# A perceiver block on one core: the sums' spread set later in its step, and a tail with loads on GpSimd, shared eT copies and split feed-forward products

## The chip, the cores and the metric

One core of a Trainium2 chip runs the whole block. The metric is the device time of one launch in microseconds. Three runs of the kernel before gave 1708.46 us in the median (1707.39 to 1709.91). In this text PE is the matrix engine (TensorE), DVE is VectorE, ACT is ScalarE, POOL is GpSimd, and SP is the engine that only issues transfers; "SPq" marks its queue.

## The reference

Eight batches of 64 latents of width 512 pass through cross attention to 1601 context rows (16 heads of 128), causal self attention over the latents (16 heads of 32) and a gated feed-forward with ternary weights. The residual sums carry through.

```python
def xattn(h, enc):                      # h: (8, 64, 512), enc: (8, 1601, 256)
    q, k, v = heads(h @ Wq), heads(enc @ Wk), heads(enc @ Wv)
    q, k = rmsnorm(q, gq), rmsnorm(k, gk)
    a = softmax(einsum('bqhd,bkhd->bhqk', q, k) / sqrt(128))
    return einsum('bhqk,bkhd->bqhd', a, v).reshape(B, S, -1) @ Wo

def attn(x):                            # causal, 16 heads of 32
    q, k, v = split(x @ w_attn + b_attn)
    a = softmax(where(tril, q @ k.T * 32 ** -0.5, -inf))
    return (a @ v) @ w_proj + b_proj

def ffn(x):
    gate, up = split(x @ ternary(w_gate_up).T)
    return rms_norm(silu(gate) * up) @ ternary(w_proj).T

x = x + xattn(layernorm(x), ctx)
x = x + attn(layernorm(x))
x = x + ffn(layernorm(x))
```

## The kernel before

**The loop.** The long middle part, from about 125 to 1398 us, is a loop of 16 *units* (eight batches times two groups of eight heads), each of six *steps* (`step(u, q)`, q from 0 to 5). A step takes two tiles of 128 context rows, makes their keys and scores by Strassen-like products (`product`, line 573, on the PSUM tiles `p_u`, `p_5`, `s_a`, `p_2`, `s_2`), and meanwhile finishes the softmax of the unit before and weighs the context with it (`weigh_context`, line 668, PSUM `y0`, `y1`). The order of the instructions of PE, DVE, ACT and POOL in this loop is the order in which they stand in the program. In the sixth step the row sums of the unit before are complete: `find_sum` (line 676) splits `den` into `denh` (ACT) and `denl` (DVE), and `spread_sum` (line 682) multiplies both by a matrix of ones on PE (line 110, PSUM `bp`) and copies the result to `rB` (ACT). `invert_sums` (DVE) takes its reciprocals later in the step. Before, `spread_sum` stands behind `tail_scores` (line 526, PSUM `sp`) and ahead of `p_5`. `bp`, `p_5` and `p_2` share the PSUM tag `m`, which has two buffers.

**The tail of cross attention** (lines 955 to 1004). Here only PE's order is written by hand; the order on the other engines and queues is the planner's. PE weighs the last unit's 13 context tiles (line 668). Their loads `cxn` (line 159) go out on SP, five buffers deep, each when PE has finished with a buffer. SP also issues 16 `wo` loads of 256 KB (line 733), `wa_qk` of 2 MB (line 989), `x_again` of 1 MB (line 971) and two `wa_vp` of 1 MB (lines 993 and 996).

**Self attention** (from line 1212). `t` counts four tiles of 128 latents (two batches each), `rp` two pairs of heads' quarters. A list `todo` holds filler work for PE with a rough cost in us: output projections of cross attention (`op`, line 754), `turn` (transposes of the normalised rows, line 1079, copied to `xT_a`), `queries_and_keys` (`mm_qk`, line 1100), `own_values` (`mm_v`, line 1118). `fill(us)` runs as much of it as the number says. The eight attention pieces (t, rp) run between: `own_scores` (`spa`, line 1136; softmax on DVE and ACT, line 1161), `own_weighted` (transposes `tp_e`, line 1184; copies `eT` on ACT, line 1186; products `oTp`, line 1193), `own_projection` (copy `oT`, line 1203; `mm_p`, line 1207; sum `x2` on DVE, line 1211). Transposes take the PSUM tag `m` (two buffers), scores `k` (two), projections and values `s` (two).

**The feed-forward.** `split_turn` normalises a tile of `x2`, transposes it and keeps it as `xT_f` (ACT, fp32r) and `xT_lo` (DVE, the rest). `gate_or_up` (line 1315, PSUM `gu`) multiplies 128 rows of the gate or up weights by both, eight matmuls for each. Sixteen rounds `r` follow, then the output products `fop` (line 1383), scaled and added in `fy` (line 1399) and stored by SP (line 1402). The weights `fgu` and `fp` are loaded from POOL's queue (2 MB each).

Of the kernel before, what the change touches and what calls it, by code (L numbers as in the profile page):

```python
# [14 lines left out]
ALU = mybir.AluOpType  # L15
# [13 lines left out]
def perceiver_kernel(  # L29
# [700 lines left out]

    def load_wo(h):
        wo_sb[h] = piece("wo", h in (0, H - 1))
        nc.sync.dma_start(wo_sb[h], wo[ts(h, HD), :])

    def values(h, tag):
        g, hg = divmod(h, HG)
# [48 lines left out]
    def step(u, q):  # L785
# [43 lines left out]
            exponentials(u - 1, js)  # L829
        if q == NQU - 1:  # L830
            tail_scores(u)
            if u > 0:
                spread_sum(u - 1)


        p_5 = bank("p_5")
# [7 lines left out]
        product(s_a[:, 0], s1, v1, True)  # L844
        product(s_a[:, 1], a11, q11, False)
        nc.scalar.copy(half[:, 1:3], s_a)
        product(p_u, s2, t2_, False)
        u2 = kept("u2")
        nc.scalar.copy(u2, p_u)
# [105 lines left out]
    with tc.manual_schedule(engines={mybir.EngineType.PE}):  # L955

        later.pop()()
        wv_sb.append(load_wv(1))
        for jw in range(NJ - LAG, NJ):
            load_contexts((last - 1) * NJ + jw + CXN)  # L960
            weigh_context(last - 1, jw)
        find_max(last)
        mB[last] = spread_diag(mB[last])
        finish(last - 1)
        for h in range(HG // 2):
            values(h, "k")
# [4 lines left out]
        nc.sync.dma_start(x_sb, xf.rearrange("(t p) d -> p t d", p=P))  # L971
# [17 lines left out]
        nc.sync.dma_start(  # L989
            wa_qk, w_attn[:, 0 : 2 * D].rearrange("(c p) n -> p c n", p=P)  # L990
        )
        wa_vp = big.tile([P, 2, ND, D], F32, tag="A", name="wa_vp")
        nc.sync.dma_start(
            wa_vp[:, 0], w_attn[:, 2 * D :].rearrange("(c p) n -> p c n", p=P)
        )
        nc.sync.dma_start(wa_vp[:, 1], w_aproj.rearrange("(c p) n -> p c n", p=P))
        finish(last)


        x1 = x_sb  # L1000
        ops = {0: ps.tile([P, D], F32, tag="s", name="op")}
        project(ops[0], 0, range(HG))
        for h in range(HG, H):
            values(h, "k")
# [65 lines left out]
            nc.vector.tensor_tensor(x1[:, t, :], ops.pop(t), x_sb[:, t, :], ALU.add)  # L1070
            xns[t] = normalise(x1, t, aw_)

    def turn(t, hi, lo=None):


        xn = xns.pop(t)
        tp = ps.tile([P, ND, P], F32, tag="m", name="tp_ln")
        for c in range(ND):
            nc.tensor.transpose(tp[:, c, :], xn[:, ts(c, P)], ident)
        if lo is None:  # L1080
            nc.scalar.copy(hi[:, :, ts(t, P)], tp)
        else:
            nc.scalar.copy(hi[:, :, ts(t, P)], tp)
            for c in range(ND):
                nc.vector.tensor_tensor(
                    lo[c][:, ts(t, P)],
                    tp[:, c, :],
                    hi[:, c, ts(t, P)].bitcast(F32),
                    ALU.subtract,
                )  # L1090
# [21 lines left out]
            ALU.add,  # L1112
        )

    def own_values(t):
        mm = ps.tile([P, D], F32, tag="s", name="mm_v")
        for c in range(ND):
            nc.tensor.matmul(
                mm,
                xT_a[:, c, ts(t, P)],  # L1120
                wa_vp[:, 0, c, :],
                start=(c == 0),
                stop=(c == ND - 1),
            )
        nc.vector.tensor_tensor(v_sb[:, t, :], mm, bv, ALU.add)

    probs, oTp = {}, {}

# [46 lines left out]
    def own_weighted(t, rp):  # L1175
# [4 lines left out]
        for r in rs:  # L1180
            e = probs.pop((t, r))
            tp = ps.tile([P, ND, P], F32, tag="m", name="tp_e")
            for j in range(ND):
                nc.tensor.transpose(tp[:, j, :], e[:, j, :], ident)
            eT[r] = aw_.tile([P, ND, P], F32, tag="eT", name="eT")
            nc.scalar.copy(eT[r], tp)
        yield
        if rp == 0:
            oTp[t] = ps.tile([P, ND, P], F32, tag="y0", name="oTp", bufs=1)
# [23 lines left out]
    with tc.manual_schedule(engines={mybir.EngineType.PE}):  # L1213
# [53 lines left out]
        put(0.0, load_fgu, 1)  # L1267
        put(3.4, own_values, 3, name="v3")

        def split_turn(t):  # L1270
            xns[t] = normalise(x2, t, aw_)
            turn(t, xT_f, xT_lo)

        pieces = [divmod(i, 2) for i in range(2 * NTT)]

        def scores_of(i):
            if i < len(pieces):
                if pieces[i][0] > 1:
                    need(f"qk{pieces[i][0]}")
                own_scores(*pieces[i])  # L1280

        scores_of(0)
        for i, (t, rp) in enumerate(pieces[:-2]):
            fill(2.0)
            scores_of(i + 1)
            fill(1.5)
            if t:
                need(f"v{t}")
            run(own_weighted(t, rp), 1.5)
            if i == len(pieces) - 3:  # L1290
                scores_of(i + 2)
            if rp == 1:
                run(own_projection(t), 1.5)
        need("v3")

        xT_f = blk([P, ND, NT], "xT_f", FR)
        xT_lo = [
            piece("xT_lo", False, FR) for _ in range(ND)
        ]
        xs_ = [xT_f[:, c, :] for c in range(ND)], xT_lo  # L1300
        load_fgu(NF // 8 + 1)
        for t in range(NTT - 2):
            put(0.5, split_turn, t)
        t = NTT - 1
        run(own_weighted(t, 0), 0.5)
        fill(1e9)
        run(own_weighted(t, 1), 0.5)
        split_turn(t - 1)
        run(own_projection(t), 0.5)

        def gate_or_up(gu, i, r, cols):
            rr = r + i * NF
            for c in range(ND):
                for n_ in range(2):
# [38 lines left out]

        acc = aw_.tile([P, NT], F32, tag="oT", name="acc", bufs=1)
        for r in range(NF):
            gu = gu0
            if r:
                gu = [ps.tile([P, NT], F32, tag=n_, name="gu") for n_ in ("k", "s")]  # L1360
                for i in range(2):
                    gate_or_up(gu[i], i, r, slice(0, NT))
# [13 lines left out]
                    load_fp(k)  # L1376
        for t in range(NTT):
            op = ps.tile([P, D], F32, tag="m", name="fop")
            for r in range(NF):

                w_r = fp_sb[r // 8][:, r // 4 % 2 * 4 : r // 4 % 2 * 4 + 4, r % 4, :]
                for n_ in range(2):
                    nc.tensor.matmul(  # L1383
                        op,
                        hT[r][n_][:, ts(t, P)],
                        w_r,
                        start=(r == 0 and n_ == 0),
                        stop=(r == NF - 1 and n_ == 1),
                    )
            if t == 0:  # L1390
                ss = ps.tile([P, NTT], F32, tag="y0", name="ss", bufs=1)
                for k in range(NTT):
                    nc.tensor.matmul(
                        ss[:, k : k + 1], acc[:, ts(k, P)], ones, start=True, stop=True
                    )
                inv = small.tile([P, NTT], F32, tag="inv", name="inv", bufs=1)
                rsqrt_into(inv, ss, 1.0 / FF, eps32_t)
            y = t2([P, D], "fy")
            nc.vector.scalar_tensor_tensor(
                y, op, inv[:, t : t + 1], x2[:, t, :], ALU.mult, ALU.add  # L1400
            )
            nc.sync.dma_start(outf[ts(t, P), :], y)


# [41 lines left out]
```

## Time and profile before

| | |
|---|---|
| median of three runs | 1708.46 us |
| the profiled run | 1706.96 us |
| its span | 1705.1 us |
| PE busy in 400 to 500, 500 to 600 us | 100.00, 99.51 |
| PE busy in 1418 to 1430 (12 us) | 10.28 |
| PE busy in 1514 to 1583 (69 us) | 66.51 |
| PE busy in 1583 to 1619 (36 us) | 30.05 |
| DMA engines busy, moved, in 1418 to 1430 | 0.92, 321 GB/s |
| DMA engines busy, moved, in 1491 to 1514 | 0.00, 0 GB/s |

A line of the timeline gives the start in us from the span's start, the length, the engine, the line of the program, the operation, the tiles written and read, the shape, how many, and in brackets how long the engine sat idle before it and what released it. The records of neighbouring matmuls overlap, because they are pipelined: a list that gives starts says more about PE's pace than the lengths. "Waits" lines give the waiting engine and line, what it waited for, the total us, how many times, and the longest.

### The profile page before, as it was taken

What the parts mean: (1) busy time and instruction counts of PE and PEld (TensorE: products, weight loads), DVE (VectorE), ACT (ScalarE), POOL (GpSimd) and SP (SyncE); (2) the same over time, 40 slices, a digit from 0 to 9 for tenths busy, and PEclk for the clock granted to TensorE, in tenths of its full rate; (3) what the DMA queues carried; (4) which work ended last, traced back from release to release, by engine and by line L of the source; (5) the groups of instructions that cost most, each with busy time, mean ns of one, the idle gap of its engine ahead of it and who ended that gap; (6) DMA issues with size and microseconds to landing.
All of it is one profiled execution on the core that took longest, in us unless ns stands there. A gap on an engine that the chain in (4) does not pass through costs nothing.

```text
span 1705.1 us, 19635 instructions
## 1 busy us (share of the span) xinstructions
PE 1675.0 (98%) x5288; PEld 929.4 (55%) x5288; DVE 1185.2 (70%) x1896; ACT 1148.2 (67%) x4487; POOL 413.0 (24%) x538
## 2 busy tenths in 40 slices
PE   8999999999999999999999999999999999999899
PEld 3445455555555555555555555555555554466687
DVE  4446778787888878787878787888878785145431
ACT  4448787878787777777787878787777763023441
POOL 1001232324232323132232324232333120100031
PEclk9999999999999999999999999999999999999999
DMA  7002122212221122222222212221121126400330
GB/s 213 1 0 41 28 51 45 47 41 53 44 52 41 41 55 43 47 43 48 47 44 45 47 41 53 44 52 41 41 55 49 46 71 232 108 0 1 99 99 25
DMA packets 257623, 92.59 MB, mean 54 GB/s; under 512 B 210128, under 2 KB 236264, under 8 KB 257512
## 3 DMA queue, kind: packets, MB, share of 16 engines
q1 hardware_dynamic: 250698, 78.48, 19.8%
q0 software_dynamic: 6240, 12.58, 2.8%
q8 instruction: 42, 0.69, 0.2%
q14 instruction: 69, 0.57, 0.1%
q10 hardware_dynamic: 574, 0.27, 0.1%
HBM read 77.62 MB, written 7.34 MB: 50 GB/s over the span
## 4 chain that ended last, share of the span: by engine, by line
PE 92%; DVE 4%; ACT 2%; DMA 1%; issue 0%; SPq 0%; DVEq 0%
PE y L668 20%; PE p_u L573 19%; PE p L573 14%; PE s_a L573 14%; PE gu L1315 3%; PE qps L346 3%; PE op L754 3%; PE s L573 2%; PE fop L1383 2%; PE mm_qk L1100 2%; PE vp L739 2%; PE kp L262 2%; PE aps L372 2%; PE sp L526 1%; PE bp L110 1%; ACT e L1161 1%
## 5 line engine op out<-in xcount | busy, mean ns | idle before, releaser
L577 ACT ACTIVATE c<-c 128x128 f32<-128x128 f32 x1152 | 340.7, 297 | 140.4 <-DVE c L874 58.5
L668 PE MATMUL y<-s,cxn 128*128 128x512 f32 x768 | 356.7, 592 | 1.7 <-DMA cxn<-in_ctx_dram 1.7
L668 PEld LDWEIGHTS y<-s,cxn 128*128 128x128 f32 x768 | 144.7, 190 | 153.1 <-issue 136.6
L577 ACT ACTIVATION_READ_ACCUMULATOR c<-c 128x1 f32 x1152 | 215.5, 187 | 0.0
L655 POOL TENSOR_TENSOR den<-den,s 128x512 f32<-128x512 f32 x150 | 190.8, 1272 | 43.4 <-ACT s L646 36.4
L573 PEld LDWEIGHTS s_a<-aT,cxS 128*128 128x128 f32 x576 | 109.3, 190 | 137.9 <-issue 123.3
L573 PE MATMUL s_a<-aT,cxS 128*128 128x256 f32 x576 | 171.3, 379 | 0.0
L862 POOL COPY gate<-mx 128x1 f32<-128x1 f32 x60 | 11.1, 185 | 618.3 <-DVE mx L561 287.1
L547 DVE TENSOR_TENSOR s<-s,ssq 128x1024 f32<-128x1024 f32 x96 | 116.9, 1218 | 24.3 <-ACT ssq L105 24.2
L646 ACT ACTIVATE s<-s,zero_t 128x1024 f32<-128x1024 f32 (+1 forms) x117 | 115.9, 991 | 4.6 <-DVE s L642 4.6
L642 DVE TENSOR_TENSOR s<-s,mB 128x1024 f32<-128x1024 f32 (+1 forms) x117 | 116.5, 1018 | 2.2 <-ACT mB L620 2.1
L563 DVE TENSOR_TENSOR mx<-mx,s 128x512 f32<-128x512 f32 x160 | 111.1, 694 | 7.6
L874 DVE TENSOR_TENSOR c<-p_u,p 128x512 f32<-128x512 f32 x96 | 65.4, 681 | 71.4 <-PE p_u L573 71.4
L899 DVE TENSOR_TENSOR s<-s_a,half 128x512 f32<-128x512 f32 x96 | 66.2, 690 | 58.7 <-POOL den L655 41.0
L577 ACT ACTIVATE p_u<-p_u 128x128 f32<-128x128 f32 x384 | 99.9, 260 | 9.1
L573 PE MATMUL p_u<-wkS,cxT 128*128 128x512 f32 x192 | 98.3, 594 | 2.6 <-DVE c L874 2.6
L573 PE MATMUL p_u<-wkS,cxS 128*128 128x512 f32 x192 | 98.2, 593 | 0.4 <-ACT p L810 0.4
L573 PE MATMUL p<-wk,cxS 128*128 128x512 f32 x192 | 98.3, 594 | 0.0
L573 PE MATMUL p<-wkS,cxS 128*128 128x512 f32 x192 | 98.2, 593 | 0.0
L573 PE MATMUL p_u<-wk,cxS 128*128 128x512 f32 x192 | 98.0, 592 | 0.0
L573 PE MATMUL p<-wk,cxT 128*128 128x512 f32 x192 | 98.0, 592 | 0.0
L573 PE MATMUL p_u<-wk,cxT 128*128 128x512 f32 x192 | 98.0, 592 | 0.0
(202 smaller groups left out, 3164.3 us busy)
## 6 DMA issues: line engine op xcount, KB each, us to landing
cxn<-in_ctx_dram SPq DMA_DIRECT2D x192, 128.0 KB
cxB<-in_ctx_dram SPq DMA_DIRECT2D x192, 64.0 KB
wf<-in_L_ffn_w_gate_up_dram SPq DMA_DIRECT2D x32, 256.0 KB
fgu<-fw POOLq DMA_DIRECT2D x4, 2048.0 KB, 8.5
fw<-wT SPq DMA_DIRECT2D x192, 32.0 KB
wq<-in_L_xattn_Wq_dram SPq DMA_DIRECT2D x4, 1024.0 KB
wf<-in_L_ffn_w_proj_dram SPq DMA_DIRECT2D x16, 256.0 KB
wo<-in_L_xattn_Wo_dram SPq DMA_DIRECT2D x16, 256.0 KB
```

What stands on the lines that cost most here:

```text
L346: nc.tensor.matmul(qps, wq_sb[h // 4][:, c, ts(h % 4, HD)], xT[:, c, :], start=(c == 0), stop=(c == ND - 1),)
L547: nc.vector.tensor_tensor(flat, flat, kr.unsqueeze(2).to_broadcast([P, 2 * HG, S]), ALU.mult)
L563: nc.vector.tensor_tensor(mx[u][:r], mx[u][:r], s[:r], ALU.max)
L573: nc.tensor.matmul(out_, a, w, start=start, stop=True, skip_group_check=not start)
L577: nc.scalar.activation(k[:, ts(h, HD)], k[:, ts(h, HD)], AF.Square, accum_out=ssq[:, 4 * half + h : 4 * half + h + 1],)
L642: nc.vector.tensor_tensor(t, t, m.to_broadcast([r, len(js), W]), ALU.subtract)
L646: nc.scalar.activation(t, t, AF.Exp, bias=zero_t[: t.shape[0]], scale=1.0)
L655: eng.tensor_tensor(den[u][:r], den[u][:r], s[:r], ALU.add)
L668: nc.tensor.matmul(yps[u][c], cxn[u, j][:r, ts(c, P)], s[:r], start=(j == 0), stop=(j == NJ - 1),)
L754: nc.tensor.matmul(op, o_sb[h][:, ts(t, P)], wo_sb[h], start=(h == 0), stop=(h == H - 1),)
L874: nc.vector.tensor_tensor(c22, p_u, p5, ALU.add)
L899: nc.vector.tensor_tensor(quarters[:, 1::2], s_a, half[:, 0:2], ALU.add)
```

## The change

1. In the sixth step `spread_sum` moves from behind `tail_scores` to behind the first `s_a` products and their copy `half`.
2. `wo`, `x_again`, `wa_qk` and both `wa_vp` are loaded from POOL's queue instead of SP's.
3. `turn(0)` and `turn(1)` run ahead of the last pair of heads of `out_projection(2)`. `own_values(2)` is cut into two halves of 256 columns, with `turn(3)` between them.
4. Of the two `eT` copies of a piece, the second goes to DVE.
5. The last three attention pieces are written out by hand: all remaining filler runs ahead of piece (2,1); scores of (3,1) stand between the transposes and the products of (2,1); the turns of feed-forward tiles 0 and 1 stand in the projection of tile 2; and the products of the first two feed-forward rounds (`first(r, i, a, e)`: round r, gate or up i, column tiles a to e) run in pieces of 128 and 256 columns between the last attention steps. `turn(2)` uses the PSUM tag `y1`.
6. The last output tile is made in two halves of 256 columns, each scaled and stored by itself.

```diff
     def load_wo(h):
-        nc.sync.dma_start(wo_sb[h], wo[ts(h, HD), :])
+        nc.gpsimd.dma_start(wo_sb[h], wo[ts(h, HD), :])
...
         if q == NQU - 1:
             tail_scores(u)
-            if u > 0:
-                spread_sum(u - 1)
...
         product(s_a[:, 0], s1, v1, True)
         product(s_a[:, 1], a11, q11, False)
         nc.scalar.copy(half[:, 1:3], s_a)
+        if u > 0 and q == NQU - 1:
+            spread_sum(u - 1)
         product(p_u, s2, t2_, False)
...
-        nc.sync.dma_start(x_sb, xf.rearrange("(t p) d -> p t d", p=P))
+        nc.gpsimd.dma_start(x_sb, xf.rearrange("(t p) d -> p t d", p=P))
...
-        nc.sync.dma_start(
+        nc.gpsimd.dma_start(
             wa_qk, w_attn[:, 0 : 2 * D].rearrange("(c p) n -> p c n", p=P)
...
-    def turn(t, hi, lo=None):
+    def turn(t, hi, lo=None, tag="m"):
...
-    def own_values(t):
-        mm = ps.tile([P, D], F32, tag="s", name="mm_v")
+    def own_values(t, cols=slice(0, D)):
+        mm = ps.tile([P, D], F32, tag="s", name="mm_v")[:, cols]
...
-            nc.scalar.copy(eT[r], tp)
+            (nc.vector.tensor_copy if r % 2 else nc.scalar.copy)(eT[r], tp)
...
         for h in PAIRS[: HG // 2]:
+            if h[0] == HG - 2:
+                turn(0, xT_a)
+                turn(1, xT_a)
             out_projection(2, h)
-        turn(0, xT_a)
-        turn(1, xT_a)
...
-        put(3.4, own_values, 2, name="v2")
+        put(1.7, own_values, 2, slice(0, D // 2))
         put(0.5, turn, 3, xT_a)
+        put(1.7, own_values, 2, slice(D // 2, D), name="v2")
...
-        for i, (t, rp) in enumerate(pieces[:-2]):
+        for i, (t, rp) in enumerate(pieces[:-3]):
...
-            if i == len(pieces) - 3:
-                scores_of(i + 2)
...
-        load_fgu(NF // 8 + 1)
-        for t in range(NTT - 2):
-            put(0.5, split_turn, t)
-        t = NTT - 1
-        run(own_weighted(t, 0), 0.5)
-        fill(1e9)
-        run(own_weighted(t, 1), 0.5)
-        split_turn(t - 1)
-        run(own_projection(t), 0.5)
+        fill(2.0)
+        scores_of(6)
+        fill(1e9)
...
-        gu0 = [ps.tile([P, NT], F32, tag=n_, name="gu") for n_ in ("k", "s")]
-        for i in range(2):
-            gate_or_up(gu0[i], i, 0, slice(0, t * P))
-        split_turn(t)
-        for i in range(2):
-            gate_or_up(gu0[i], i, 0, slice(t * P, NT))
+        def first(r, i, a, e):
+            if (r, i) not in gus:
+                gus[r, i] = ps.tile([P, NT], F32, tag="ks"[i], name="gu")
+            gate_or_up(gus[r, i], i, r, slice(a * P, e * P))
+
+        gus = {}
+        for t in range(2):
+            xns[t] = normalise(x2, t, aw_)
+        w = own_weighted(2, 1)
+        next(w)
+        scores_of(7)
+        next(w, None)
+        o = own_projection(2)
+        next(o)
+        for t in range(2):
+            turn(t, xT_f, xT_lo)
+        next(o, None)
+        xns[2] = normalise(x2, 2, aw_)
+        w = own_weighted(3, 0)
+        next(w)
+        first(0, 0, 0, 2)
+        next(w, None)
+        w = own_weighted(3, 1)
+        next(w)
+        turn(2, xT_f, xT_lo, "y1")
+        first(0, 1, 0, 2)
+        next(w, None)
+        o = own_projection(3)
+        next(o)
+        first(1, 0, 0, 2)
+        next(o, None)
+        load_fgu(NF // 8 + 1)
+        xns[3] = normalise(x2, 3, aw_)
+        for i in range(2):
+            first(0, i, 2, 3)
+        first(1, 1, 0, 2)
+        turn(3, xT_f, xT_lo)
+        for i in range(2):
+            first(0, i, 3, 4)
+        for i in range(2):
+            first(1, i, 2, 4)
...
+            n_parts = 2 if t == NTT - 1 else 1
+            for part in range(n_parts):
+                cols = ts(part, D // n_parts)
...
+                nc.vector.scalar_tensor_tensor(
+                    y[:, cols],
+                    op[:, cols],
...
+                nc.sync.dma_start(outf[ts(t, P), cols], y[:, cols])
```

`next(w)` runs a generator up to its `yield`, that is, the transposes and copies of `own_weighted` or the copy of `own_projection`; the second `next` runs the products behind it.

More of the change, by code (lines that the diff above doesn't have):

```diff
@@ L992, in perceiver_kernel @@
         wa_vp = big.tile([P, 2, ND, D], F32, tag="A", name="wa_vp")
-        nc.sync.dma_start(
+        nc.gpsimd.dma_start(
             wa_vp[:, 0], w_attn[:, 2 * D :].rearrange("(c p) n -> p c n", p=P)
         )
-        nc.sync.dma_start(wa_vp[:, 1], w_aproj.rearrange("(c p) n -> p c n", p=P))
+        nc.gpsimd.dma_start(wa_vp[:, 1], w_aproj.rearrange("(c p) n -> p c n", p=P))
         finish(last)
@@ L1071, in out_projection @@
             xns[t] = normalise(x1, t, aw_)
-    def turn(t, hi, lo=None):
+    def turn(t, hi, lo=None, tag="m"):
         xn = xns.pop(t)
-        tp = ps.tile([P, ND, P], F32, tag="m", name="tp_ln")
+        tp = ps.tile(
+            [P, ND, P], F32, tag=tag, name="tp_ln", bufs=1 if tag == "y1" else None
+        )
         for c in range(ND):
@@ L1120, in own_values @@
                 xT_a[:, c, ts(t, P)],
-                wa_vp[:, 0, c, :],
+                wa_vp[:, 0, c, cols],
                 start=(c == 0),
@@ L1124, in own_values @@
             )
-        nc.vector.tensor_tensor(v_sb[:, t, :], mm, bv, ALU.add)
+        nc.vector.tensor_tensor(v_sb[:, t, cols], mm, bv[:, cols], ALU.add)
     probs, oTp = {}, {}
@@ L1268, in perceiver_kernel @@
         put(3.4, own_values, 3, name="v3")
-        def split_turn(t):
-            xns[t] = normalise(x2, t, aw_)
-            turn(t, xT_f, xT_lo)
         pieces = [divmod(i, 2) for i in range(2 * NTT)]
         def scores_of(i):
[L1277 to L1280, printed above, removed]
+            if pieces[i][0] > 1:
+                need(f"qk{pieces[i][0]}")
+            own_scores(*pieces[i])
         scores_of(0)
-        for i, (t, rp) in enumerate(pieces[:-2]):
+        for i, (t, rp) in enumerate(pieces[:-3]):
             fill(2.0)
@@ L1289, in perceiver_kernel @@
             run(own_weighted(t, rp), 1.5)
-            if i == len(pieces) - 3:
-                scores_of(i + 2)
             if rp == 1:
                 run(own_projection(t), 1.5)
-        need("v3")
+        fill(2.0)
+        scores_of(6)
+        fill(1e9)
         xT_f = blk([P, ND, NT], "xT_f", FR)
-        xT_lo = [
-            piece("xT_lo", False, FR) for _ in range(ND)
-        ]
+        xT_lo = [piece("xT_lo", False, FR) for _ in range(ND)]
         xs_ = [xT_f[:, c, :] for c in range(ND)], xT_lo
-        load_fgu(NF // 8 + 1)
-        for t in range(NTT - 2):
-            put(0.5, split_turn, t)
-        t = NTT - 1
-        run(own_weighted(t, 0), 0.5)
-        fill(1e9)
-        run(own_weighted(t, 1), 0.5)
-        split_turn(t - 1)
-        run(own_projection(t), 0.5)
         def gate_or_up(gu, i, r, cols):
@@ L1357, in perceiver_kernel @@
         for r in range(NF):
-            gu = gu0
-            if r:
+            gu = [gus.get((r, i)) for i in range(2)]
+            if r > 1:
                 gu = [ps.tile([P, NT], F32, tag=n_, name="gu") for n_ in ("k", "s")]
@@ L1378, in perceiver_kernel @@
             op = ps.tile([P, D], F32, tag="m", name="fop")
[L1379 to L1397, printed above, removed]
@@ L1398, in perceiver_kernel @@
-            y = t2([P, D], "fy")
[L1399 to L1402, printed above, removed]
+            y = t2([P, D], "fy")
+            n_parts = 2 if t == NTT - 1 else 1
+            for part in range(n_parts):
+                cols = ts(part, D // n_parts)
+                for r in range(NF):
+                    k0 = r // 4 % 2 * 4 + part * (4 // n_parts)
+                    w_r = fp_sb[r // 8][:, k0 : k0 + 4 // n_parts, r % 4, :]
+                    for n_ in range(2):
+                        nc.tensor.matmul(
+                            op[:, cols],
+                            hT[r][n_][:, ts(t, P)],
+                            w_r,
+                            start=(r == 0 and n_ == 0),
+                            stop=(r == NF - 1 and n_ == 1),
+                        )
+                if t == 0:
+                    ss = ps.tile([P, NTT], F32, tag="y0", name="ss", bufs=1)
+                    for k in range(NTT):
+                        nc.tensor.matmul(
+                            ss[:, k : k + 1],
+                            acc[:, ts(k, P)],
+                            ones,
+                            start=True,
+                            stop=True,
+                        )
+                    inv = small.tile([P, NTT], F32, tag="inv", name="inv", bufs=1)
+                    rsqrt_into(inv, ss, 1.0 / FF, eps32_t)
+                nc.vector.scalar_tensor_tensor(
+                    y[:, cols],
+                    op[:, cols],
+                    inv[:, t : t + 1],
+                    x2[:, t, cols],
+                    ALU.mult,
+                    ALU.add,
+                )
+                nc.sync.dma_start(outf[ts(t, P), cols], y[:, cols])
```

## The prediction

> **What bounds the kernel now.** I read the page's busy times and chain first, then who TensorE waits for, then the timeline at those places.
>
> ```profile
> PE 1675.0 (98%) x5288; PEld 929.4 (55%) x5288; DVE 1185.2 (70%) x1896; ACT 1148.2 (67%) x4487; POOL 413.0 (24%) x538
> PE 92%; DVE 4%; ACT 2%; DMA 1%; issue 0%; SPq 0%; DVEq 0%
> ```
>
> TensorE is the bound almost everywhere: the chain that ends last is PE for 92% of the span, at a granted clock of 1.00 (0.98 only in the last 56 us). So a part of the change is worth what it takes out of PE's idle time, plus or minus PE work. TensorE's waits name the idle time:
>
> ```profile
> PE oTp L1193 <- ACT eT L1186: 3.6, 3, 1.8
> PE bp L110 <- DVE denl L132: 3.1, 7, 0.5
> PE tp_ln L1079 <- ACT eT L1186: 1.8, 1, 1.8
> PE y L668 <- DMA cxn<-in_ctx_dram: 1.7, 1, 1.7
> PE mm_qk L1100 <- ACT xT_a L1081: 1.4, 2, 0.7
> ```
>
> (Columns: total us, times, longest.) These understate the losses. Matmul records overlap: fp32 512-wide ones last 0.59 us but start 0.43 apart, so a PE that runs dry looks busy while it drains. I therefore count starts: the start that follows without a gap, against the real one. Unit prices by starts: fp32 512-wide 0.43, 256-wide 0.215; fp32r 512-wide 0.231, 384-wide 0.173, 128-wide 0.111; a 128-wide transpose 0.11; 16 `spa` 1.09, 16 `oTp` 1.00.
>
> **Part 1, the sums' spread.** The timeline at the sixth step of two neighbouring units:
>
> ```profile
> 348.02 0.80 PE L110 MATMUL bp<-denh,ones_r 128*128 128x512 f32 x1
> 348.51 0.69 DVE L132 TENSOR_TENSOR denl<-den,denh 128x512 fp32r<-128x512 f32 x1
> 349.25 0.50 PE L110 MATMUL bp<-denl,ones_r 128*128 128x512 f32 x1 [0.44 <-DVE denl L132]
> 349.60 1.02 PE L573 MATMUL p<-wkS,cxS 128*128 128x512 f32 x2
> 428.12 0.69 DVE L132 TENSOR_TENSOR denl<-den,denh 128x512 fp32r<-128x512 f32 x1
> 428.31 0.79 PE L110 MATMUL bp<-denh,ones_r 128*128 128x512 f32 x1
> 428.94 0.42 PE L110 MATMUL bp<-denl,ones_r 128*128 128x512 f32 x1
> 429.20 1.02 PE L573 MATMUL p<-wkS,cxS 128*128 128x512 f32 x2
> ```
>
> In the first, VectorE makes `denl` late, and from `denh` to the next product are 1.58 us; in the second 0.89. The difference, 0.69 to 0.70, is lost in 7 of the 15 units. The period confirms it: from one `denh` to the next it is 79.60 us or, after a late one, 80.29. The change sets two 512-wide and four 256-wide products (2 x 2 x 0.43 / 2 for each half: 0.86 + 0.86 = 1.72 us) ahead of `bp`. `denl` ends 1.2 us after `denh` starts, so the wait is covered. **7 x 0.70 = -4.9.** Nothing else becomes late: the copy `rB` moves from 349.8 to about 350.9 on ScalarE, while VectorE's reciprocals that need it stood 4.8 us behind it (274.25 against 269.50); behind it in ScalarE's queue is `u2`, whose product ends 0.9 us after `bp`, longer than the 0.59 of `rB`. `bp`, `p_5` and `p_2` rotate through two buffers, so `p_2` now takes the one of `p_5`, which `c12` frees at 273.70 against a start at 276.61. If that cover failed it would cost up to 0.7 in each of 15 units, +10; against it stands the 2.9 us. Ends: -4.9 to 0.
>
> **Part 2, loads on GpSimd.** SP holds the loads and `cxn` in one line:
>
> ```profile
> 1418.27 0.38 SPq L989 DMA_DIRECT2D wa_qk<-in_L_attn_w_attn_dram  x1
> 1419.13 0.38 SPq L971 DMA_DIRECT2D x_again<-in_x_dram  x1
> 1420.85 7.19 SPq L159 DMA_DIRECT2D cxn<-in_ctx_dram  x5
> ...
> 1429.40 12.26 PE L668 MATMUL y<-s,cxn 128*128 128x512 f32 x28 [1.72 <-DMA cxn<-in_ctx_dram]
> ```
>
> The sixth `cxn` goes out at 1420.85, when PE has freed its buffer, behind 3 MB, and PE restarts at 1429.40. Without a gap it would be 1418.93 + 20 x 0.43 = 1427.53: 1.87 lost. Moved to another queue, the 3 MB no longer stand ahead of 128 KB. All 20 moved issues count: 16 `wo`, `x_again`, `wa_qk`, two `wa_vp`; POOL's issue of `fgu` takes 0.90 (median), so at most 18 us in a stretch in which POOL does nothing (0 busy in 1400 to 1450). `wo` no longer waits behind the five `cxn` issues (7.19). The masks and `fgu` behind them are wanted at 1512 and from about 1595 on. The transfer itself has little room: the DMA engines were busy 0.92 at 321 GB/s in 1418 to 1430. Ends: -1.9 (no stall) to +15 (the slow rival below). Nearest rows, `fgu` at 2 MB in 8.5 us from this queue, say it keeps its rate: I take **-1.9**.
>
> The Trainium skill ("DMA: Bandwidth & Descriptors", Rules for kernel authors) speaks against this: loads spread over issuing engines gain no bandwidth, since all use the same 16 DMA engines. By that rule this term is 0; its section Queues, rings and completion order says each engine takes turns between queues, which would give -1.9. No run here has yet had both queues loaded.
>
> **Part 3, attention in the tail.** Turns 0 and 1 ahead of the last two projection heads: transposes end at 1491.74 + 8 x 0.11 = 1492.63, `mm_qk` starts 1493.50; the two copies (1.07) now hide behind 1.72 of projections, and `xn` was ready at 1487.95. **-0.9.** Turn 3 between the halves of `own_values(2)` (16 x 0.215, the same PE time): 1571.03 + 0.47 against 1572.36, **-0.9**. First `oTp`: two `eT` copies in one queue, the second behind eight exponentials:
>
> ```profile
> 1521.04 0.56 ACT L1186 COPY eT<-tp_e 128x512 f32<-128x512 f32 x1
> 1523.06 0.56 ACT L1186 COPY eT<-tp_e 128x512 f32<-128x512 f32 x1
> 1523.68 1.06 PE L1193 MATMUL oTp<-eT,v_sb 128*32 128x128 f32 x14 [1.48 <-ACT eT L1186]
> ```
>
> 16 `oTp` from 1521.79 should end at 1522.79; they end at 1524.67. VectorE was idle for 0.40 before 1521.16 and its like copy (L750) takes 0.69, so the second copy is there by 1521.8: **-1.9**. Ends of the three: -3.7 to 0.
>
> **Part 4, the last attention steps and first products.** From the end of the sixth `tp_e` (1586.53 + 0.87 = 1587.40) to the end of the second `gu` pair (1615.25 + 16 x 0.231 = 1618.95) PE takes 31.55. The work of the new order: scores 1.09, three `oTp` 3.00, two `tp_e` 1.74, turns 0.90 + 0.45 + 0.45, two `mm_p` 6.86, `gu` in 128-wide pieces 32 x 0.111 = 3.55, in 256-wide pieces 48 x 0.115 = 5.52: 23.56. So 8.0 is the most. A 256-wide fp32r product is not in the trace; between 0.111 (128-wide) and 0.173 (384-wide) I take half of 512-wide, 0.115; the upper end costs 2.8. What stays idle: the sixth `oTp` waits for the first `eT`, which ScalarE reaches after the exponentials of step (3,0) at 1588.77 + 0.55, when PE has finished the scores at 1588.49: 0.9. The same pattern at (3,0), with 3.1 us of exponentials ahead and 0.92 of `gu` as cover: about 1.2. Before turn 3 the chain add, statistics, two ACT steps, `xn` lasted from 1608.49 to 1611.89, 3.4, against 1.78 + 0.92 of cover and pipeline drain: 0.5. After it `xT_f` and the first `xT_lo`: 0.85 + 0.25. Together 3.7, so 8.0 - 3.7 = **-4.3**, ends -8.0 to +1 (nothing hidden, pieces dear, VectorE late: in the 7.3 us after 1587.40 it has to make two normalised `e` 1.75, an `eT` 0.69, the next `e` and maxima 2.85, eight `xT_lo` 1.76: 7.05). `fgu` 3 goes out after the last projection as before (1609.07).
>
> **Part 5, the end.** The last output group in two halves: 64 x 0.115 against 32 x 0.231, level (upper end 0.173: +3.7). The last `fy` falls from 0.75 towards the 0.42 of a 256-wide VectorE row, and half of 256 KB at 321 GB/s leaves 0.4 less to store: -0.75. Against it, the second half may have to wait until `fy` has read the first out of the same PSUM tile: 0.1 + 0.45 + 0.1: +0.65. I take **-0.1**, ends -0.75 to +3.7.
>
> The Trainium skill ("PSUM — Partial Sum Buffer", PSUM bank collisions raise a hardware error) has TensorE and a reader kept apart by bank, whatever the columns. By it the wait is there and the end gains 0.1; without it 0.75. The trace has no such pair.
>
> **Sum.** -4.9 - 1.9 - 0.9 - 0.9 - 1.9 - 4.3 - 0.1 = -14.9. The profiled run took 1706.96 us (span 1705.1 and 1.86 around it): 1692.1. The median of the runs shown is 1.5 higher, 1708.46, so for it I say **1693.6**.
>
> **Rivals.** Times are for the median.
> - *Only the loop gains.* The tail's waits move: exponentials stay ahead of `eT` in ScalarE's queue, pieces are dear, VectorE takes over as last. For it: VectorE's load above, and only PE's order is written by hand there. Against: turns 0, 1 and 3 need no such luck. 1708.46 - 4.9 = 1703.6. Chance 0.08.
> - *The change doesn't do in the loop what it says:* `bp` is late for another reason. For: nothing but that only 7 units show it. Against: the period. 1693.6 + 4.9 = 1698.5. Chance 0.04.
> - *Slower: `cxn` starves.* With `wo`, `wa_qk` and `wa_vp` (8 MB) free to go early on another queue, a `cxn` load takes L instead of 8.42. Five buffers: the sixth tile is issued 1.92 after the stage starts and wanted at 8.6, stall L - 6.7; the eleventh likewise L - 6.9. To be slower by 0.2% these must exceed the 1.87 of now, the other gains of 13.0 and 3.4: 2L - 13.6 = 18.3, L from 16, twice today's. At L = 17: 1708.46 + 20.4 - 1.87 - 13.0 = 1714.0. For it: the 0.92 DMA share. Against: 128 KB at 321 GB/s are 0.4 us. Chance 0.06.
> - In between, gains and losses cancel (L about 14): no change. Chance 0.04.
>
> The forecast holds 0.78. About 0.2%, 3.4 us, is what a measurement of this kernel can tell from no change; forecast and first two rivals lie beyond it: faster 0.90, same 0.04, slower 0.06. Range: all idle gone, the better end and the spread of the runs give 1688; dear pieces (2.8 + 3.7), or part 4 at nothing, reach 1700; I stop at 1702, just short of the first rival.
>
> **What would show it.** Right: no `bp` wait and every unit period 79.6; no `y` wait for `cxn`; `eT` copies 8 on ACT, 8 on DVE; `oTp` waits for `eT` under 2.5 in all; the second `gu` pair ending some 4 earlier counted from the sixth `tp_e`. Wrong: a `cxn` or `wo` wait above 2 us, a new wait of `p_2` for `c12`, 256-wide `gu` starts 0.15 or more apart.

## The result, and the profile after

The changed kernel takes **1697.47 us** (median of 4 runs, 1695.35 to 1699.65), the kernel before on the same chip 1709.18; the ratio is 0.9932, 95% interval 0.9915 to 0.9949. Predicted were 1693.6 with a range of 1688 to 1702. The profiled execution took 1695.35 us (span 1693.6, before 1705.1): 11.5 less in the span, where the sum of the prediction said 14.9.

Two lines of the page of the changed kernel, busy times and the shares of the chain that ended last:

```profile
PE 1673.2 (99%) x5360; PEld 935.6 (55%) x5360; DVE 1189.4 (70%) x1906; ACT 1141.8 (67%) x4479; POOL 424.2 (25%) x558
PE 96%; ACT 2%; DVE 2%; DMA 0%; issue 0%; SPq 0%; DVEq 0%
```

TensorE's share of the chain rose from 92 to 96%, VectorE's fell from 4 to 2, the DMA's from 1 to 0: what went out was idle time of TensorE, and nothing else took the lead. The waits of TensorE (total us, times, longest), of which `bp`, `y` and `mm_qk` are no longer a part:

```profile
PE kp L262 <- DMA wk<-in_L_xattn_Wk_dram: 3.8, 1, 3.8
...
PE oTp L1195 <- DVE eT L1188: 0.7, 1, 0.7
PE oTp L1195 <- ACT eT L1188: 0.7, 1, 0.7
...
PE gu L1307 <- ACT xT_f L1085: 0.7, 1, 0.7
PE fop L1415 <- DVE fy L1434: 0.6, 1, 0.6
PE tp_ln L1081 <- DVE xn L123: 0.4, 1, 0.4
```

The `oTp` waits for `eT` fell from 3.6 to 1.4 us. In the timeline of the changed kernel (start, length, engine, line, operation, tiles; in brackets the idle time before it) the places shown ahead of the prediction now read so, from the sums' spread over the `y` block and the first `oTp` to the step (3,0) and the last output tile:

```profile
351.80 0.58 PE L110 MATMUL bp<-denh,ones_r 128*128 128x512 f32 x1
352.21 0.39 PE L110 MATMUL bp<-denl,ones_r 128*128 128x512 f32 x1
...
1415.94 20.88 PE L668 MATMUL y<-s,cxn 128*128 128x512 f32 x48
...
1515.97 1.24 PE L1195 MATMUL oTp<-eT,v_sb 128*32 128x128 f32 x16
...
1586.96 0.68 DVE L1213 TENSOR_TENSOR x<-mm_p,x_again 128x512 f32<-128x512 f32 x1
...
1587.55 0.68 DVE L1172 TENSOR_TENSOR e<-e,d 128x512 f32<-128x512 f32 x1
...
1588.15 0.69 DVE L117 BATCH_NORM_STATS2 st<-x 128x6 f32<-128x512 f32 x1
...
1588.34 0.41 PE L1195 MATMUL oTp<-eT,v_sb 128*32 128x128 f32 x2
1588.75 0.68 DVE L1188 COPY eT<-tp_e 128x512 f32<-128x512 f32 x1
...
1589.48 1.06 PE L1195 MATMUL oTp<-eT,v_sb 128*32 128x128 f32 x14 [0.74 <-DVE eT L1188]
...
1685.52 0.48 DVE L1434 SCALAR_TENSOR_TENSOR fy<-fop,inv,x 128x256 f32<-128x256 f32 x1 [3.06 <-PE fop L1415]
...
1686.06 4.08 PE L1415 MATMUL fop<-fp,hT 128*128 128x256 f32 x32 [0.65 <-DVE fy L1434]
```

The second `bp` starts 0.41 behind the first, and from one `bp` of `denh` to the next it is now 79.57 to 79.67 us in all units of the loop. The 48 `y` run in one piece, and the first 16 `oTp` are one group without a wait. Two losses are left for the text below: at (3,0) VectorE makes `eT` as the last of four instructions, and the second half of the last output tile waits 0.65 for `fy` to have read the first.

Where the 11.5 us come from, read off as differences of starts. The landmarks are starts in the timelines, before and after: the first and the last `sp`, `tp_mx` of the last unit, the first `op`, the first and the second `mm_v`, the scores of (3,0), the first `fy`, the span's end.

| stretch | before | after | difference | predicted |
|---|---|---|---|---|
| start to first `sp` | 189.57 | 191.43 | +1.9 | 0 |
| first to last `sp` (the loop) | 1196.84 | 1191.99 | -4.9 | -4.9 |
| last `sp` to `tp_mx` | 17.63 | 17.61 | 0.0 | 0 |
| to the first `op` (the loads) | 39.63 | 37.81 | -1.8 | -1.9 |
| to the first `mm_v` (turns 0, 1) | 63.75 | 62.76 | -1.0 | -0.9 |
| to the second `mm_v` (first `oTp`) | 17.25 | 15.54 | -1.7 | -1.9 |
| to the scores of (3,0) (turn 3) | 57.10 | 56.23 | -0.9 | -0.9 |
| to the first `fy` (last attention steps, first products) | 99.04 | 95.43 | -3.6 | -4.3 |
| to the span's end | 24.31 | 24.77 | +0.5 | -0.1 |

(Some expectations below take the first `op` from the chain of waits, 0.16 later, so 39.80 for the 39.63 here, and count the loop to the last of its four `sp`, 1.3 later. What was measured is given by starts as here. In the changed kernel and the six others with its loads, the stretch of the loads takes 37.8 to 38.2.)

The +1.9 at the start is no work of the change: nothing of the diff runs there. The first `kp` waits for its weights 1.5 to 4.2 us, and starts between 7.12 and 9.45 us, in the 14 kernels profiled here, whose beginnings are alike; in the run before it happened to start at 7.43, after at 8.93. That is 1.5 of the 1.9. From there to the first `sp` the 14 kernels take 182.0 to 183.3 us, which holds the rest.

### The profile page after: what moved, and what is told of

The parts are those of the page before. It is cut to its first block, busy times and chain, and to the rows that moved or that the text cites. A ratio compares the mean times of both kernels' runs of the same rounds, so it can differ in the third digit from the quotient of the medians.

```text
span 1693.6 us, 19783 instructions
## 1 busy us (share of the span) xinstructions
PE 1673.2 (99%) x5360; PEld 935.6 (55%) x5360; DVE 1189.4 (70%) x1906; ACT 1141.8 (67%) x4479; POOL 424.2 (25%) x558
## 4 chain that ended last, share of the span: by engine, by line
PE 96%; ACT 2%; DVE 2%; DMA 0%; issue 0%; SPq 0%; DVEq 0%
PE y L668 21%; PE p_u L573 19%; PE s_a L573 14%; PE p L573 14%; PE gu L1307 3%; PE qps L346 3%; PE op L754 3%; PE s L573 2%; PE fop L1415 2%; PE mm_qk L1102 2%; PE vp L739 2%; PE sp L526 2%; PE kp L262 2%; PE aps L372 2%; PE mm_v L1120 1%; PE bp L110 1%
```

## The experiments

In all of them the changed stretch is compared, not the whole time alone, since the start alone moves a single run by 2 us.

### The spread alone

```diff
         if q == NQU - 1:
             tail_scores(u)
-            if u > 0:
-                spread_sum(u - 1)
...
         nc.scalar.copy(half[:, 1:3], s_a)
+        if u > 0 and q == NQU - 1:
+            spread_sum(u - 1)
```

> The kernel before with the sums' spread moved alone. My theory: in 7 of 15 units PE loses 0.70 us because denl is late, and 1.72 us of products ahead of bp cover it. From the first to the last start of the tail scores' products (line 526) there were 1198.1 us before and 1193.3 after the whole change; here again 1193.2 to 1193.4, so 4.8 to 4.9 less, every unit period 79.6, and the rest of the span as before. Rival: the loop's gain in the whole change came from the loads, which leave SP's queue; then it is 1198.1 here. Second rival: only the idle time that the waits show is given back, 3.1 us, 1195.0.

Measured: the loop took 4.9 us less, as in the changed kernel, and no wait of `bp` is left; over ten runs the median is 1705.54 us, ratio 0.9980 (0.9970 to 0.9989), an interval that takes in the 4.9 (0.9971). The first step of the sum is shown. The profiled span alone, 1703.4, fell by 1.7 only: the start took 0.8 more, and the stretch from the scores of (3,0) to the first `fy` 2.3 more (101.35 against 99.04), which the last section explains.

### The loads: which line the small ones stand in

All 20 loads on GpSimd and nothing else changed (five lines from `nc.sync.dma_start` to `nc.gpsimd.dma_start`, of which the diff ahead of the prediction shows three):

> The kernel before with all 20 loads of the tail on GpSimd's queue, nothing else. My theory: the stretch from the transposes of the maxima (tp_mx) to the first output projection (op), 39.80 us before and 37.97 after the whole change, is 38.0 here: the wait of y for cxn is gone and nothing else in the stretch changes. From there to the end nothing changes (261 us). Rival: it needs the other parts of the change, and the stretch stays at 39.8. Slow rival: wo or x_again come too late without the other parts, and op waits for a load by 1 us or more.

Measured: 37.99 us from `tp_mx` to `op`, the 48 `y` in one piece. Part 2 alone gives 1.6 us, where the changed kernel has 1.8. That nothing changes behind it did not come true in this execution: from `op` to the end are 264.13 us instead of 261.45, as the granted clock was 0.66 over 1590 to 1600 (see the last section). So the one time of this kernel, 1709.65 us, shows nothing of the gain; the stretch does.

Only the two loads that stood ahead of `cxn` (`wa_qk`, `x_again`) on GpSimd, `wo` and `wa_vp` still on SP:

> The kernel before with only wa_qk and x_again (3 MB) on GpSimd's queue; wo and wa_vp stay on SP with cxn. My theory: the sixth cxn was late because these 3 MB stood ahead of it in its own queue; with them in the other queue the stretch from tp_mx to op is 38.0 to 38.3. Rival: what counts is how much is in flight on the 16 DMA engines in all, or that SP's queue is free of the wo loads; then the stretch stays near 39.8.

That expectation failed: the stretch took **43.78** us, 4.15 longer than in the kernel before. TensorE and SP's queue in its timeline:

```profile
1422.39 0.38 SPq L993 DMA_DIRECT2D wa_vp<-in_L_attn_w_attn_dram  x1
1424.11 2.04 SPq L159 DMA_DIRECT2D cxn<-in_ctx_dram  x2
1426.25 0.86 SPq L733 DMA_DIRECT2D wo<-in_L_xattn_Wo_dram  x2
1427.55 0.33 SPq L159 DMA_DIRECT2D cxn<-in_ctx_dram  x1
1427.92 0.43 SPq L996 DMA_DIRECT2D wa_vp<-in_L_attn_w_proj_dram  x1
...
1435.11 13.95 PE L668 MATMUL y<-s,cxn 128*128 128x512 f32 x28 [4.17 <-DMA cxn<-in_ctx_dram]
```

With two loads gone, the order in which SP issues came out anew: `wa_vp` and pairs of `wo` now stand between the `cxn`, and another 3 MB run beside them in GpSimd's queue. `y` waits 4.17 us where it waited 1.72. That is 2.4 of the 4.15. The other 1.7 is the granted clock, which was 0.79, 0.50 and 0.86 in the three windows of 2 us from 1434 on: the 28 `y` behind the wait take 13.95 us and not 12.26. So either the line itself makes `y` wait, or the two queues at work together do. The changed kernel with its last `cxn` on GpSimd as well, so that everything stands in one line:

```diff
-            load_contexts(last * NJ + j + CXN)
+            load_contexts(last * NJ + j + CXN, nc.gpsimd)
```

(likewise one call earlier, with an argument for the engine handed down to the load)

> The whole change with the tail's cxn loads on GpSimd's queue too, so that one queue holds everything again, wa_qk and x_again ahead of the sixth cxn. My theory (a queue serves its transfers in turn, two queues share the engines): the y products wait for cxn again, by 1.5 us or more, and the stretch from tp_mx to op grows from 37.97 to 39.5 or more; cxn lands 7 us or more after its issue. Rival (GpSimd's queue is simply served better, or the DMA engines have room): the stretch stays at 38.0.

```profile
1426.68 12.25 PE L668 MATMUL y<-s,cxn 128*128 128x512 f32 x28 [2.54 <-ACT denh L131]
```

Measured: 40.44 us, and a gap of 2.54 in `y`. The bracket names `denh`, of which `y` reads nothing; the `cxn` loads took 2.4 to 9.0 us to land there, and the sixth, issued at 1417.58, landed at 1426.55, 0.13 before `y` goes on. In one line with the large loads the wait is back, whichever engine issues them.

Next, the kernel before with `wa_qk`, `x_again` and both `wa_vp` on GpSimd, so that of the large loads only `wo` is left on SP:

> The kernel before with `wa_qk`, `x_again` and both `wa_vp` on GpSimd, the 16 `wo` left on SP. It settles why two loads moved made the stretch from `tp_mx` to the first `op` longer (43.78 against 39.80). My theory now: SP's own order then put the 2 MB of `wa_vp` ahead of `cxn`; with `wa_vp` in the other queue nothing larger than `wo` (256 KB) stands in SP's line, and the stretch is 37.9 to 38.8. Rival (two queues at once halve the rate that `cxn` gets, whatever stands in its line): `y` waits again for `cxn`, 40 or more.

The expectation failed again, and by more. TensorE's `y` and SP's queue in its timeline:

```profile
1424.62 0.91 SPq L733 DMA_DIRECT2D wo<-in_L_xattn_Wo_dram  x2
1425.91 2.04 SPq L159 DMA_DIRECT2D cxn<-in_ctx_dram  x2
1428.05 0.97 SPq L733 DMA_DIRECT2D wo<-in_L_xattn_Wo_dram  x2
1430.59 2.38 SPq L159 DMA_DIRECT2D cxn<-in_ctx_dram  x2
...
1430.66 3.68 PE L668 MATMUL y<-s,cxn 128*128 128x512 f32 x8 [1.34 <-DMA cxn<-in_ctx_dram]
1438.53 10.52 PE L668 MATMUL y<-s,cxn 128*128 128x512 f32 x20 [4.19 <-DMA cxn<-in_ctx_dram]
```

The stretch took 45.39 us, 5.5 of it in two waits, and another 1.8 is the clock again: 20 `y` take 10.52 us behind the second wait, where 20 take 8.75 in the kernel before. Pairs of `wo` (512 KB) stand between the `cxn`, and 5 MB run beside them in the other queue. In the changed kernel the 5 MB of the other four loads do not go out together: `wo` waits on GpSimd for buffers that `y` frees and holds `wa_vp` behind it until 1427.84 and 1434.74. Whether that holding back or the absence of `wo` from SP's line is what spares it, the last run of the series tells: the changed kernel with `wo` issued behind `wa_vp`.

```diff
-        for h in range(H):
-            load_wo(h)
         wa_qk = big.tile([P, ND, 2 * D], F32, tag="A", name="wa_qk")
...
         nc.gpsimd.dma_start(wa_vp[:, 1], w_aproj.rearrange("(c p) n -> p c n", p=P))
+        for h in range(H):
+            load_wo(h)
```

> The changed kernel with the 16 `wo` issued behind `wa_vp` in GpSimd's line: SP still holds nothing but `cxn` there, while `wa_qk`, `x_again` and both `wa_vp` (5 MB) can go out together, no longer held back by `wo` loads that wait for their buffers. Two readings are left of the run with four loads moved, where `y` waited 5.5 us for `cxn`. First (pace): while several MB stream in another queue, `cxn` is slowed whatever stands in its own line, and the changed kernel is spared only since its `wo` hold `wa_vp` back: `y` waits for `cxn` again, 1 us or more, stretch from `tp_mx` to the first `op` 39 to 44. Second (own line): `cxn` waited for the 512 KB pairs of `wo` ahead of it on SP: here no `y` wait above 0.3, stretch 37.9 to 38.3. I hold the second for somewhat likelier, 0.55, as in the changed kernel 3 MB already stream beside `cxn` without a wait.

The `y` block and the queues of GpSimd and SP in its timeline:

```profile
1396.46 33.19 SPq L159 DMA_DIRECT2D cxn<-in_ctx_dram  x11
...
1414.98 21.61 PE L668 MATMUL y<-s,cxn 128*128 128x512 f32 x48
...
1416.19 0.75 POOL L991 DMA_DIRECT2D wa_vp<-in_L_attn_w_attn_dram  x1
1416.93 0.75 POOL L994 DMA_DIRECT2D wa_vp<-in_L_attn_w_proj_dram  x1
```

All 5 MB are issued by 1417.7, and the 48 `y` still run in one block (21.61 us; 20.88 in the changed kernel, 21.07 with all loads moved alone). The stretch is 38.52 us against 37.8 to 38.2: between the two bands that were set, but with no `cxn` wait listed. So what streams in the other queue costs 0.3 to 0.7 by itself, in this one execution, and nearly all of the waiting in the runs with two and with four loads moved came with large loads in SP's own line. For the two waits of 4.2 us they stood ahead of the `cxn`. For the wait of 1.34 with four loads moved they did not: that `cxn` went out at 1422.48, the last load ahead of it on SP at 1405.90, and the first `wo` pair followed at 1424.62. It took 8.2 us until `y` went on, where its like here, issued at 1416.89 beside the same 5 MB, was there within 6.7. Why it was later no run shows. That `wo` moved too is no ornament of the change but a condition of its gain.

### The eT copies and the turns

All `eT` copies of the changed kernel on ScalarE:

```diff
-            (nc.vector.tensor_copy if r % 2 else nc.scalar.copy)(eT[r], tp)
+            nc.scalar.copy(eT[r], tp)
```

> The changed kernel with all `eT` copies on ScalarE. My theory: the first `oTp` waits again, so that from the last scores ahead of it to `mm_v` 1.5 to 1.9 us come back; in the last attention steps (2,1) and (3,0) little changes, since there VectorE's copy was as late as ScalarE's would be (-0.9 to +0.6); together +1 to +2.5 us. Rival (PE's order alone gives the gain, the copies' engine does not matter): under 0.5 at both places. As the wait of some 1.8 us is back, the granted clock after it may fall below 0.9 for some 5 us, as in three runs so far.

TensorE at the first `oTp` in its timeline, to be held against the single group at 1515.97 above:

```profile
1515.93 0.41 PE L1195 MATMUL oTp<-eT,v_sb 128*32 128x128 f32 x2
1517.81 1.06 PE L1195 MATMUL oTp<-eT,v_sb 128*32 128x128 f32 x14 [1.47 <-ACT eT L1188]
```

From the scores (`spa`) ahead of it to `mm_v` it took 8.99 against 7.29 us: +1.70, the whole of that term. At (2,1), from `tp_e` to `tp_ln`, 4.33 against 3.86: +0.47. At (3,0), from its `tp_e` to the last projection `mm_p`, 7.36 against 8.58: **-1.22**. In sum +0.95, a little under what was expected; the whole times (1696.02, 4 runs) can't tell it from the changed kernel's. The fall of the clock that was held possible did not come: it stayed at 1.00 throughout the tail. The split of the copies is right at the first place and wrong at (3,0).

Turns 0 and 1 behind all projections again, `own_values(2)` whole ahead of turn 3:

```diff
-            if h[0] == HG - 2:
-                turn(0, xT_a)
-                turn(1, xT_a)
             out_projection(2, h)
+        turn(0, xT_a)
+        turn(1, xT_a)
...
-        put(1.7, own_values, 2, slice(0, D // 2))
+        put(3.4, own_values, 2, name="v2")
         put(0.5, turn, 3, xT_a)
-        put(1.7, own_values, 2, slice(D // 2, D), name="v2")
```

> The changed kernel with turns 0 and 1 behind all projections again, and `own_values(2)` whole ahead of turn 3. My theory: the waits of `mm_qk` for `xT_a` are back at both places, 0.9 each: the stretch from the last scores' product to the second `tp_e` of step (2,1) is longer by 1.7 to 1.9, two waits `mm_qk` <- ACT `xT_a` of some 0.7 are listed. Rival (the next wait would have come anyway, so that a turn's place gives nothing): under 0.5 in all.

Two lines of TensorE in its timeline:

```profile
1486.75 14.08 PE L1102 MATMUL mm_qk<-xT_a,wa_qk 128*128 128x256 f32 x64 [0.73 <-ACT xT_a L1083]
...
1563.90 2.05 PE L1102 MATMUL mm_qk<-xT_a,wa_qk 128*128 128x128 f32 x16 [0.67 <-ACT xT_a L1083]
```

Both waits are back. From the first `op` to `tp_e` of (2,1) it took 141.59 against 139.29 us: 2.30 more, where 1.7 to 1.9 were expected. The first turn is worth 0.89 (`op` to `mm_qk`, 49.83 against 48.94). Of the rest, 0.4 is in 16 `oTp` behind the second (1568.54 to 1569.97, 1.43 where such a group takes 1.00), which had not been thought of.

### The end, and the two remedies together

The last output tile whole again (`n_parts = 1`):

> The changed kernel with the last output tile as one group again. My theory: the two halves cost more than they save: from the first `fop` of the last weight block to the span's end the changed kernel takes 34.9 us, the kernel before 34.4; here 34.3 to 34.5, the wait of `fop` for `fy` (0.65) gone, the last `fy` back at 0.75, all else as in the changed kernel (loop 1193.3). Rival (the halves help, and the 0.6 comes from elsewhere in the output products): 35.3 or more.

From the first `fy` of the output to the span's end: 24.26 us (before 24.31, changed kernel 24.77), median 1696.46, ratio 0.9924 (0.9905 to 0.9943). The wait is gone, and 0.51 with it. (The stretch named in the expectation, from the first `fop` of the last block, is 34.6 against 35.1.)

The halves kept, the second in a PSUM tile of its own:

```diff
             for part in range(n_parts):
                 cols = ts(part, D // n_parts)
+                if part:
+                    op = ps.tile([P, D], F32, tag="k", name="fop")
```

> The changed kernel with the second half of the last output tile in a PSUM tile of its own. My theory: the second half waits only because `fy` reads the same tile: the 0.65 wait is gone, the same stretch is 34.2 to 34.4, and starts of the 256-wide products stay 0.115 to 0.125 apart. Rival (the second half waits for something else, such as the 64 weights' loads or `inv`): the wait stays above 0.4, the stretch at 34.9.

TensorE's last groups and the last two `fy` in its timeline:

```profile
1664.89 22.58 PE L1417 MATMUL fop<-fp,hT 128*128 128x512 f32 x128
...
1683.77 0.48 DVE L1436 SCALAR_TENSOR_TENSOR fy<-fop,inv,x 128x256 f32<-128x256 f32 x1 [3.07 <-PE fop L1417]
1687.51 0.48 DVE L1436 SCALAR_TENSOR_TENSOR fy<-fop,inv,x 128x256 f32<-128x256 f32 x1 [3.26 <-PE fop L1417]
```

No wait is left, and TensorE's products are one group. The stretch from the first `fy` is 23.87: 0.91 under the changed kernel and 0.39 under the whole tile. So halves do pay, 0.39 us on balance, once the second half does not share a tile with what `fy` reads.

Two kernels join a remedy at the end with one at (3,0), where both `eT` are made on ScalarE. The first has the whole last tile, the second the two PSUM tiles:

```diff
-            (nc.vector.tensor_copy if r % 2 else nc.scalar.copy)(eT[r], tp)
+            (nc.vector.tensor_copy if r % 2 and (t, rp) != (NTT - 1, 0) else nc.scalar.copy)(
+                eT[r], tp
+            )
```

> The changed kernel with the last output tile whole, and in the step (3,0) both `eT` copies on ScalarE. My theory: at (3,0) VectorE made its copy last of four instructions (0.74 of wait and the drain of TensorE); ScalarE is free then and makes it by 1.1 earlier: the second part of these `oTp` starts 0.8 to 1.0 sooner. With the end, 1.3 to 1.6 us below the changed kernel: a ratio to the kernel before near 0.992. Rival (the next step is bound by something else and the 0.9 is lost again before the second `gu` pair ends): only the 0.5 of the end.

> The changed kernel with both `eT` of step (3,0) on ScalarE, and the last output tile in halves with a PSUM tile each. My theory: both gains add: from `tp_e` of (3,0) to `tp_ln` of turn 3 15.5 to 15.7 (changed kernel: see there 15.31 longer by 1.0), from the first 512-wide `fy` to the span's end 23.8 to 24.0 (24.8 in the changed kernel): together 1.9 to 2.0 below the changed kernel; ratio to the kernel before 0.990. Rival: the gains share a cause and do not add: 1.0 or less.

| | changed | whole end + `eT` | two tiles + `eT` |
|---|---|---|---|
| `tp_e` of (3,0) to `tp_ln` of turn 3 | 15.31 | 14.29 | 14.30 |
| first `fy` to the span's end | 24.77 | 24.28 | 23.86 |
| median us | 1697.47 (4 runs) | 1693.21 (4 runs) | 1694.68 (5 runs) |
| ratio to before | 0.9932 (0.9915 to 0.9949) | 0.9903 (0.9886 to 0.9919) | 0.9912 (0.9895 to 0.9930) |

The gains add in the trace: -1.0 at (3,0) in both, -0.5 or -0.9 at the end. (The stretch at (3,0) is 14.3, not the 15.5 to 15.7 that the second expectation wrote, which had set the longer figure for the shorter; the difference to the changed kernel is what it said.) Both medians lie below the changed kernel's, but the intervals of the ratios overlap, so a better version is shown by its stretches and not by its whole time. By its stretches the second is the best, 1.9 us under the changed kernel.

## Why the prediction was right, by its steps

**Part 1** held to the tenth: 7 times 0.70 in the loop, and the spread alone gives it. `p_2` got no wait for `c12`.

**Part 2** gave -1.8 for -1.9. But its reason, "Moved to another queue, the 3 MB no longer stand ahead of 128 KB", was half of the matter: with only these 3 MB moved `y` waited 4.2 us, 2.4 more than before, and the stretch got 4 us longer with the clock's 1.7. Of the ways tried, only the move of all the large loads out of SP's line took the wait away. The prediction had counted `wo` only as a cost on GpSimd and as freed from waiting, and not as something that would come to stand ahead of `cxn`. The rival in which `cxn` starves did not come to pass in the changed kernel, and the runs with two and with four loads moved show that its mechanism is at hand: stalls of 4.2 and 5.5 us, with `cxn` and large loads in one line while a second queue is full. The two sections of the Trainium skill that were weighed there ("DMA: Bandwidth & Descriptors") had given 0 and -1.9 for this term; the measured -1.8 agrees with the turns between queues (Queues, rings and completion order), though no trace here shows the turns themselves. The bandwidth rule is not contradicted by it: the gain needs only that the `cxn` arrive earlier, and no higher rate.

**Part 3**: turns 0 and 1 -1.0, turn 3 -0.9, first `oTp` -1.7, each predicted within 0.2, and each taken back by its own undoing (0.9, 1.4, 1.7).

**Part 4** was mis-sized, -3.6 for "8.0 - 3.7 = -4.3". From the end of the sixth `tp_e` to the end of the second `gu` pair are 27.97 us (1579.00 to 1606.97), where 23.56 + 3.7 = 27.26 had been reckoned. The idle places were right and their sum was even smaller, from the starts: 0.80 at (2,1), 1.01 at (3,0), 0.55 before turn 3, 0.85 and 0.22 behind it, 3.43 together. What failed is the work, "23.56": it was made of whole groups at their steady pace. The 256-wide `gu` start 0.12 apart instead of 0.115 (48 of them, 0.24), and the other 0.74 are left for the seams of the 18 groups in this stretch, where for instance the first and the second product of a 256-wide group start 0.17 to 0.22 apart. Which seam costs how much was not tried by a run. And at (3,0) the reason was another than the one given, "3.1 us of exponentials ahead" on ScalarE: ScalarE was done early, and VectorE, given the second copy, had an addition, a product and a statistic of 0.7 us each ahead of it. The move of that copy back to ScalarE takes out 1.0. The prediction's low end had named VectorE late as a danger here, and then priced the place by ScalarE.

**Part 5** was mis-sized, "-0.1" for +0.5, and all three of its sizes were off. The wait was there as set against it, 0.65 in the list, but TensorE also runs dry ahead of it and fills again behind it: from the third `fy` to the last are 8.47 us, with two tiles 7.56, so it costs 0.91 and not 0.65. The products that were called level take 0.20 more (7.56 against 7.36 for the whole tile). And the gain, "The last `fy` falls from 0.75 towards the 0.42", with the store 0.75 in all, is 0.60: from the start of the last `fy` to the span's end are 3.40 us and 4.00 with the whole tile, of which 0.27 is `fy` itself (0.48 for 0.75). Together 0.91 + 0.20 - 0.60 = +0.51, which is what the changed kernel takes more than the one with the whole tile (24.77 against 24.26). By the Trainium skill ("PSUM — Partial Sum Buffer", PSUM bank collisions raise a hardware error) the wait had been bound to come, with -0.1 for the sum instead of -0.75. It came, and a tile of its own removes it; whether the chip asks for it or only the order that the program keeps by tiles, no run here tells.

So without the start, which differs by chance, the span fell by 13.4 where 14.9 had been said; 1.3 of the 1.5 are the two terms above. The median lies 3.9 above the forecast: 1.5 by the sum, and the rest was not taken apart run by run; the start and the clock, of which the last section tells, differ by as much between executions.

## What to carry to other kernels

A small load that is due soon must not share an issuing line with large ones, and moving some of the large ones is not enough: after the move look at what the line holds now, since its order can come out anew. When copies are split between two engines, decide it place by place, by which of the two has fewer instructions ahead there; the same split gained 1.7 us at one step and lost 1.0 at another. And a tile that is cut in two to overlap its product with its reader needs two PSUM tiles, or the cut costs more than it gives; the cut by itself costs TensorE a little too, 0.20 us for the 64 half-wide products here.

## What was not expected of the hardware

**The granted clock falls to half behind short idle places, in some executions.** Windows of 2 us behind turn 3 (length, busy times of the engines, then the granted clock, the share of the DMA engines and GB/s), first of the changed kernel, where TensorE idles 0.40 and 0.68 between 1601 and 1603:

```profile
1602.00:1604.00 2.00, 1.32 (x10) 0.95 (x9) 0.88 (x4) 1.65 (x2) 0.00 (x0) 1.00 1.47 413
1604.00:1606.00 2.00, 2.00 (x19) 2.00 (x19) 0.69 (x1) 0.82 (x2) 0.00 (x0) 1.00 1.48 381
1606.00:1608.00 2.00, 2.00 (x15) 1.83 (x14) 1.00 (x2) 1.64 (x3) 0.00 (x0) 1.00 0.19 45
```

and of the kernel with two PSUM tiles and `eT` on ScalarE, with the same two waits:

```profile
1602.00:1604.00 2.00, 1.33 (x10) 1.19 (x11) 0.88 (x4) 1.87 (x2) 0.00 (x0) 1.00 1.49 408
1604.00:1606.00 2.00, 2.00 (x13) 2.00 (x13) 0.69 (x1) 0.68 (x2) 0.00 (x0) 0.64 1.37 349
1606.00:1608.00 2.00, 2.00 (x12) 2.00 (x11) 0.69 (x1) 1.55 (x3) 0.00 (x0) 0.51 0.02 4
```

The same instructions at the same distance from turn 3 run at 1.00 in one and at about 0.5 for some 3.4 us in the other (1604.54 to 1607.95). From `tp_ln` of turn 3 to the first `fy` that costs 68.67 against 67.13 us, 1.5. It happened at this place in 4 of the 9 profiled executions of the changed kernel and its variants, and cost 1.5 to 2.0 each time. In the old order of the last attention steps, with its waits of 1.82 us, it came in 3 of 5: with the spread alone (0.82 and 0.83 over 1580 to 1600), with all loads moved, and with four loads moved; there it cost 2.3, 2.7 and 5.3 us between the scores of (3,0) and the first `fy`. It also stood behind the 4.2 us waits of `y`. The profiled executions of the two kernels compared had none of it. Runs of one kernel differ by 0.7 to 7.2 us, and this is one of the causes. The Trainium skill ("TensorE: Matmul & The Clock Gate", Part 1) describes a gate that goes to half clock by a free-running window of about 3.4 us; the length and the depth here agree, and that it strikes one execution and not another fits a window that is not tied to the kernel. Its rule of thumb (section Why this matters for your kernels), no idle gap over some 3 us, is too mild for this case: the fall came in four executions behind two gaps of 1.1 us in all within 3 us. That closing the gaps would also end the fall of the clock was not tried.
